# Between two propagation steps of a graph network: two of five adjacency products ahead of the put-off tile's overflow check, and the first of them pinned behind its logits

## The chip, the cores and the metric

The kernel runs on one core of one Trainium2 chip. The metric is the device time of one launch in microseconds (us), of which lower is better. Before the change it is 3214.06 us, the median of three runs.

## What is computed

The reference is a stack of four graph layers over 4096 nodes with 256 features each; after each layer comes a residual sum and a layer norm. The change lies in the second layer, which runs two steps. Each step multiplies the features by a row-normalised adjacency matrix (`R @ Xf`), and another copy of the features by an attention matrix cut to its top 90% of mass (`A @ Xa`).

```python
for n in range(2):
    q = Xa @ W1.T @ W2.T;  k = Xa @ W3.T
    probs = softmax(q @ k.T)
    A = probs with only the largest entries kept, whose sum reaches 0.9, rows summing to 1
    Xf = R @ Xf                      # R = (adj + I), rows summing to 1
    Xa = A @ Xa
    Z = Z + Xf @ U1[n].T + Xa @ U2[n].T
h = layernorm(X + Z)
```

## The kernel before

Rows are worked on in 32 tiles of 128 (`NT` is 32). For each tile, TensorE makes the logits against all 4096 keys in 8 chunks of 512 columns (L414), and ScalarE copies each chunk out of PSUM (L415). VectorE finds the largest values of each row (L433, then `tops`), ScalarE takes the exponential (L452 or L456), and VectorE's `pick` finds the threshold that leaves 90% of the mass.

In step 0 a row is expected to keep at most 16 entries, whose source rows are gathered by number with indirect DMAs on GpSimd's queue (L672). They are summed by matmuls with diagonal weights `dg` (VectorE L759, TensorE L761). Rows that keep more than that are entered into a list in DRAM. They are handled again at the end of the step, gathered into one full tile: the **put-off tile** (`put_off`, one tile in step 0, because `LATER[0]` is 1). It goes the dense way:

1. its list is loaded (SyncE L886), turned into row numbers (VectorE L888), and its rows are gathered (GpSimd L810, `xf_new`);
2. query (L394), logits (L414, L415), maximum (L433), exponential over the whole row (ScalarE L456), the 64 largest values (L528, L532), threshold (L550 to L564), which leaves a flag `bad_l` for each row;
3. the **overflow check**: a 1x1 matmul counts the flags (TensorE L588), ScalarE copies the count (L590), VectorE loads it into a register and branches around a slow search (L647, L648);
4. after the branch `settle` zeroes one group of surplus values (L658) and everything below the threshold (L663);
5. TensorE turns the cleaned row tile in chunks (L744), ScalarE copies (L747), TensorE multiplies by the features (L767), and the result is mixed, stored, and used for the keys and queries of step 1.

For a few more rows than the put-off tile holds there is a loop with a count known only at run time (`left_over`, L928). With this input it runs zero times, but all engines meet at it.

Step 1's adjacency products can start as soon as step 0's `Xf` is complete. `load_halves` loads it back from DRAM in eight pieces (SyncE L165, VectorE L150 and L152, ScalarE L151, tile `xh`). Five of the 32 products of step 1 stand between the steps. One product (`r_product`) is 8 calls of `neighbours`: SyncE fetches an 8-bit adjacency tile that serves two calls (L681, three buffers), ScalarE casts it (L683, two buffers `adjq`), and TensorE runs four matmuls (L686). After the last call a matmul with the identity closes the product (L688), and the result leaves by ScalarE (L705), VectorE (L706) and SyncE (L712). Successive products alternate between two PSUM banks.

The kernel is written against a scheduler. It takes instructions in the written order as priorities, and gives every engine an order fixed at build time. It may move an instruction ahead of ones written before it where its model of time finds a gap. It may not move instructions across a run-time branch that was written between them, so what is written before the check stays before it on every engine. `tc.keep_in_program_order(i)` takes that freedom from one instruction: it stays behind what was written before it on its engine.

The stages of the put-off tile are a generator; `advance(job)` runs it to its next `yield`. By the time the loop over tiles ends, it has been advanced twice (rows gathered, then query and logits). In the old version the remaining stages were all run by `finish`, below the five products. The third advance holds maximum, exponential, `tops`, `pick` and the check's matmul and copy; the fourth holds the register load, the branch and L654 to L658.

Of the kernel before, what the change touches and what calls it, by code (L numbers as in the profile page):

```python
# [56 lines left out]
def gnn_stack(ctx, tc, x, adjt, adjn, w0, b0, w1, w2t, w3t, u1t, u2t, ln_g, ln_b, w2, b2, w3, b3, out):  # L57
# [3 lines left out]
    nc = tc.nc  # L61
# [295 lines left out]
    with tc.tile_pool(name="l1", bufs=1, reuse_waits="tile") as l1:  # L357

        cur = {"late": False, "n": 0, "nef_done": False}


        FIRST = [[range(k * NT // 16, (k + 1) * NT // 16) for k in range(2)]]
# [311 lines left out]

        GP = LC // P

        def neighbours(n, i, g, acc_r, pn, xf):

            if g % 2 == 0:
                cur["a8"] = cur["w"].tile([P, 2 * GP, P], F8, tag="adj8", name="adj8", bufs=3)  # L680
                nc.sync.dma_start(cur["a8"], adj8_d[i][:, g * GP : (g + 2) * GP, :])  # L681
            a = cur["w"].tile([P, GP, P], F32R, tag="adjq", name="adjq", bufs=2)
            nc.scalar.copy(a, cur["a8"][:, g % 2 * GP : (g % 2 + 1) * GP, :])  # L683
            for j in range(GP):
                jt = g * GP + j
                nc.tensor.matmul(acc_r, a[:, j, :], xf[:, jt, :], start=(jt == 0), stop=False)  # L686
            if g + 1 == NLC:
                nc.tensor.matmul(acc_r, ident_r, xf[:, i, :], start=False, stop=True)  # L688
            if pn is not None:
                if g % (NLC // 2) == 0:  # L690
                    cur["b8"] = cur["w"].tile([P, NT // 2, P], F8, tag="adjn8", name="adjn8", bufs=2)
                    nc.gpsimd.dma_start(cur["b8"], adjn[i, :, g * GP : g * GP + NT // 2, :])
                k = g % (NLC // 2) * GP
                for j in range(GP):
                    jt = g * GP + j
                    nc.tensor.matmul(pn[:, :P], cur["a8"][:, g % 2 * GP + j, :], cur["b8"][:, k + j, :], start=(jt == 0),
                                     stop=(jt == NT - 1))

        def r_acc(i):

            return ps_acc.tile([P, 512], F32, tag=("acc", "nef")[i % 2 if cur["nef_done"] else 0], name="acc_r", bufs=1)

        def r_end(i, acc_r, pn):
            xf_new = work.tile([P, D], F32, tag="xf_new", name="xf_new", bufs=1)
            nc.scalar.activation(xf_new, acc_r[:, :D], AF.Copy, scale=rs[:, i : i + 1])  # L705
            nc.vector.scalar_tensor_tensor(xf_new, acc_r[:, D:], rs[:, i : i + 1], xf_new, op0=ALU.mult, op1=ALU.add)  # L706
            if pn is not None:

                junk = spare_row.bitcast(F32)[:, :P]
                nc.vector.scalar_tensor_tensor(junk, pn[:, :P], 1.0, ident, op0=ALU.mult, op1=ALU.mult,  # L710
                                               accum_out=nef[:, i : i + 1])
            nc.sync.dma_start(rows(xf_d, i), xf_new)  # L712

        def r_product(n, i, xf):

            acc_r, pn = r_acc(i), None
            if n == 0:
                pn = ps_acc.tile([P, 512], F32, tag="nef", name="nef_ps", bufs=1)
            for g in range(NLC):
                neighbours(n, i, g, acc_r, pn, xf)  # L720
            r_end(i, acc_r, pn)

        def pieces(n, st, nxt, ops, rs_now=()):
# [27 lines left out]
            for g in range(NLC):  # L751
                if nxt is not None:
                    logits_chunk(nxt["e"], nxt["q"], g)
                if few:
                    per = KEPT // NLC
                    for k in range(g * per, (g + 1) * per):
                        if k % 4 == 0:
                            dg = cur["w"].tile([P, 4, P], F32, tag="at", name="dg", bufs=2)
                            nc.vector.tensor_mul(dg, ident[:, None, :].to_broadcast([P, 4, P]),  # L759
                                                 st["w"][:, k : k + 4, None].to_broadcast([P, 4, P]))  # L760
                        nc.tensor.matmul(acc_a, dg[:, k % 4, :], st["G"][k], start=(k == 0), stop=(k == KEPT - 1))  # L761
                elif st is not None:
                    if g + 1 < NLC:
                        turn(g + 1)
                    for j in range(G):
                        jt = g * G + j
                        nc.tensor.matmul(acc_a, ats[g][:, j, :], cur["xa"][:, jt, :], start=(jt == 0),  # L767
                                         stop=(jt == NT - 1))
                if with_r:
                    neighbours(n, i, g, acc_r, pn, cur["xf"])  # L770
                for f in ops.get(g, ()):
                    f()
            if st is None:
                for i in rs_now:
                    r_product(n, i, cur["xf"])
            else:
                xa_new = work.tile([P, D], F32, tag="xa_new", name="xa_new", bufs=1)
                nc.scalar.activation(xa_new, acc_a, AF.Copy, scale=st["sc"])
                if n + 1 < STEPS:
                    put(xa_d, st, xa_new)  # L780
                st["xa"] = xa_new
# [11 lines left out]
        def fetch(n, st):  # L793

            i = st["tile"]
            for key, src in (("xf", xf_d), ("res", h_d if n else x1_d), ("x1", x1b_d)):
                if n == 0 and (key == "x1" or key == "res" and i is not None):
                    continue
                if i is None:
                    st[key] = gathered(src, st, key)  # L800
                else:
                    st[key] = work.tile([P, D], F32, tag=key, name=key, bufs=1)
                    nc.sync.dma_start(st[key], rows(src, i))
            if n == 0 and i is not None:
                st["res"] = cur["xa"][:, i, :]
# [136 lines left out]
        def run_step(n, es):  # L942
# [6 lines left out]
            jobs = []  # L949

            def advance(job):

                cur["late"] = True
                st = next(job["stages"], "end")
                cur["late"] = False
                if st == "end":
                    return True
                if st is not None:
                    job["st"] = st
                return False  # L960
# [19 lines left out]
            for i in range(-2, NT):  # L980
# [21 lines left out]
                if 0 < i + 2 < NT - 1:  # L1002
                    turned = []
                    g = 1 if n else 6
# [40 lines left out]
            if n == 0:  # L1045
                for fs in last:
                    for f in fs:
                        f()
                last = []
                cur["late"] = True  # L1050
                fetch(n, jobs[0]["st"])
                cur["late"] = False
                cur["nef_done"] = True
                for i in range(FIRST[1][0][0]):
                    r_product(1, i, cur["next"])
            todo = []
            if n > 0:
# [172 lines left out]
```

## Time and profile before

| what | value |
|---|---|
| runs | 3208.3, 3214.06 and 3225.59 us, median 3214.06 |
| profiled execution | 3106.69 us, of which the span is 3105.0 us |
| granted TensorE clock, mean | 0.976 |
| TensorE matmul busy | 2902.2 us, 93% of the span |
| VectorE, ScalarE, GpSimd busy | 2253.7, 1725.0 and 779.8 us |
| from the end of step 0's loop to step 1's first logits | about 1187 to 1300 us of the span |

The span is the time from the first to the last instruction. "PE" is TensorE's matmuls, "PEld" its weight loads, "DVE" VectorE, "ACT" ScalarE, "POOL" GpSimd, "SP" SyncE. A name such as "DVE e L663" is the engine, the tile that is written, and the source line. The granted clock is the share of full speed at which TensorE was allowed to run.

### The profile page before, as it was taken

The numbers are of one execution on the slowest core, as the hardware profiler recorded it, in microseconds if no ns is written. First come the engines' busy times: TensorE is split into PE (matmuls) and PEld (weight loads), VectorE is DVE, ScalarE is ACT, GpSimd is POOL, SyncE is SP. The second block draws the span as 40 slices with busy tenths as digits, with TensorE's granted clock in tenths as the row PEclk, the third lists the DMA queues.
The fourth block names the chain that finished last, engine by engine and source line by source line (L and its number), as shares of the span: only waits on it lengthen the run. The fifth ranks groups of instructions, "written<-read, shape, count | busy, mean of one in ns | idle before, by whom it ended". The sixth has DMA issues, their size and how long they took to land. (4 is left out here: it accounts for less than half of the span.)

```text
span 3105.0 us, 45412 instructions
## 1 busy us (share of the span) xinstructions
PE 2902.2 (93%) x14244; PEld 2300.0 (74%) x14244; DVE 2253.7 (73%) x7159; ACT 1725.0 (56%) x2883; POOL 779.8 (25%) x908
## 2 busy tenths in 40 slices
PE   7999889999999997799999999999999978999998
PEld 3788677788878875577777877878878546777886
DVE  4666688888888884379997999959998725443444
ACT  2555566666666655364555555546554426666664
POOL 1111167777777772000000000010001110000000
PEclk9999999999999998899999999999999998999999
DMA  9996378888878873310000111101111324333332
GB/s 170 158 176 136 66 131 138 164 153 154 147 153 155 161 149 112 117 50 25 25 21 25 37 34 38 30 31 35 39 35 32 115 88 152 107 107 97 107 107 78
DMA packets 247484, 299.44 MB, mean 96 GB/s; under 512 B 34464, under 2 KB 201312, under 8 KB 247232
## 3 DMA queue, kind: packets, MB, share of 16 engines
q0 software_dynamic: 46336, 104.28, 23.8%
q1 hardware_dynamic: 188656, 180.93, 18.9%
q10 hardware_dynamic: 12240, 11.23, 1.1%
q8 instruction: 115, 1.88, 0.3%
q14 instruction: 137, 1.12, 0.2%
HBM read 330.65 MB, written 66.32 MB: 128 GB/s over the span
## 5 line engine op out<-in xcount | busy, mean ns | idle before, releaser
L686 PE MATMUL acc_r<-xh,adjq 128*128 128x512 f32 x2048 | 617.1, 430 | 20.9 <-ACT adjq L683 12.0
L767 PE MATMUL acc_bank<-xa,at 128*128 128x256 f32 x2240 | 548.1, 385 | 25.8 <-ACT at L747 25.4
L672 POOL DMA_INDIRECT G<-x_d,cols x512 | 496.6, 970 | 214.4 <-PE acc_bank L761 77.6
L683 ACT CAST adjq<-adj 128x512 fp32r<-128x512 fp8e4 x512 | 316.2, 620 | 399.5 <-PE acc_r L686 318.8
L767 PEld LDWEIGHTS acc_bank<-xa,at 128*128 128x128 f32 x2240 | 408.4, 192 | 84.3 <-ACT at L747 37.1
L686 PEld LDWEIGHTS acc_r<-xh,adjq 128*128 128x128 f32 x2048 | 378.9, 191 | 110.4 <-ACT adjq L683 31.8
L433 DVE MAX8 cand<-e 128x8 f32<-128x228 f32 (+1 forms) x1088 | 386.6, 399 | 71.1 <-ACT e L415 69.5
L199 POOL TENSOR_TENSOR rstd<-ve,mhalf 128x1 f32<-128x1 f32 x166 | 100.3, 604 | 1330.9 <-DVE ve L197 1287.5
L415 ACT COPY e<-lg 128x512 f32<-128x512 f32 x544 | 315.0, 585 | 183.7 <-PE lg L414 179.9
L414 PE MATMUL lg<-kS,q 128*128 128x512 f32 x1088 | 385.0, 439 | 0.1
L1110 ACT CAST a<-a 128x1024 fp32r<-128x1024 fp8e4 x256 | 268.1, 1049 | 167.9 <-PE acc L175 127.9
L761 PE MATMUL acc_bank<-G,dg 128*128 128x256 f32 x1024 | 272.2, 387 | 12.5 <-DMA adj<-adj_d 5.4
L530 DVE FIND_INDEX8 cols<-top,e 128x8 uint32<-128x4096 f32 x64 | 282.8, 4419 | 0.0
L175 PE MATMUL acc<-xh,a 128*128 128x512 f32 x1024 | 261.9, 410 | 21.0 <-DMA x2i<-x_d 17.1
L175 PE MATMUL acc<-y0h,a 128*128 128x512 f32 x1024 | 250.0, 398 | 0.0
L175 PEld LDWEIGHTS acc<-xh,a 128*128 128x128 f32 x1024 | 193.5, 192 | 67.7 <-ACT xh L151 22.2
L175 PE MATMUL acc<-yh,a 128*128 128x512 f32 x1024 | 237.9, 394 | 0.0
L761 PEld LDWEIGHTS acc_bank<-G,dg 128*128 128x128 f32 x1024 | 196.6, 193 | 49.5 <-DVE dg L759 10.0
L175 PEld LDWEIGHTS acc<-yh,a 128*128 128x128 f32 x1024 | 192.3, 188 | 43.6
L175 PEld LDWEIGHTS acc<-y0h,a 128*128 128x128 f32 x1024 | 188.1, 188 | 38.8 <-issue 0.6
L747 ACT COPY at<-at_ps 128x512 f32<-128x512 f32 x288 | 168.8, 588 | 83.0 <-PE at_ps L744 81.3
L414 PEld LDWEIGHTS lg<-kS,q 128*128 128x128 f32 x1088 | 180.1, 192 | 20.4 <-ACT e L415 6.4
(287 smaller groups left out, 4430.3 us busy)
## 6 DMA issues: line engine op xcount, KB each, us to landing
adj<-adj_d SPq DMA_DIRECT2D x256, 128.0 KB
a<-adj_d SPq DMA_DIRECT2D x256, 128.0 KB
a<-in_adjt POOLq DMA_DIRECT2D x64, 256.0 KB
adj_d<-a SPq DMA_DIRECT2D x64, 256.0 KB
adjn<-in_adjn POOLq DMA_DIRECT2D x64, 256.0 KB
x_d<-x SPq DMA_DIRECT2D x64, 128.0 KB
xf_d<-xf_new SPq DMA_DIRECT2D x64, 128.0 KB
xf<-xf_d SPq DMA_DIRECT2D x64, 128.0 KB
```

Source lines behind the costliest of these rows:

```text
L175: nc.tensor.matmul(acc, a[:, j, :], halves(jt), start=(jt == 0), stop=(jt == NT - 1))
L414: nc.tensor.matmul(pl[:, :LC], q[k], kS[:, s], start=(k == 0), stop=(k == 1))
L415: nc.scalar.copy(l[:, s], pl[:, :LC])
L433: nc.vector.max(dst[:, 8 * g : 8 * g + 8], src[:, g * w : min((g + 1) * w, N)])
L530: nc.vector.max_index(st["at"][:, 8 * r : 8 * r + 8], t8, st["e"][:, :N])
L672: nc.gpsimd.indirect_dma_start(out=g, out_offset=None, in_=x1_d, in_offset=bass.IndirectOffsetOnAxis(ap=st["at"][:, k : k + 1], axis=0))
L683: nc.scalar.copy(a, cur["a8"][:, g % 2 * GP : (g % 2 + 1) * GP, :])
L686: nc.tensor.matmul(acc_r, a[:, j, :], xf[:, jt, :], start=(jt == 0), stop=False)
L747: nc.scalar.copy(at[:, :G, :], ps[:, :G, :])
L761: nc.tensor.matmul(acc_a, dg[:, k % 4, :], st["G"][k], start=(k == 0), stop=(k == KEPT - 1))
L767: nc.tensor.matmul(acc_a, ats[g][:, j, :], cur["xa"][:, jt, :], start=(jt == 0), stop=(jt == NT - 1))
L1110: nc.scalar.copy(a, a8)
```

## The change

Of the five products, the first two stay ahead of the put-off tile's next two stages, and the other three are written behind these. The branch thus stands, on every engine, behind two products instead of five. The first matmul of the first product is also pinned: it may not move ahead of what was written before it, the put-off tile's logits among that.

```diff
-        def neighbours(n, i, g, acc_r, pn, xf):
+        def neighbours(n, i, g, acc_r, pn, xf, pinned=False):
...
-                nc.tensor.matmul(acc_r, a[:, j, :], xf[:, jt, :], start=(jt == 0), stop=False)
+                first = nc.tensor.matmul(acc_r, a[:, j, :], xf[:, jt, :], start=(jt == 0), stop=False)
+                if pinned and jt == 0:
+                    tc.keep_in_program_order(first)
...
-        def r_product(n, i, xf):
+        def r_product(n, i, xf, pinned=False):
...
-                neighbours(n, i, g, acc_r, pn, xf)
+                neighbours(n, i, g, acc_r, pn, xf, pinned)
...
-                for i in range(FIRST[1][0][0]):
+                early = FIRST[1][0][0]
+                for i in range(early // 2):
+                    r_product(1, i, cur["next"], i == 0)
+                for _ in range(2):
+                    advance(jobs[0])
+                for i in range(early // 2, early):
                     r_product(1, i, cur["next"])
```

`early` is 5, so `early // 2` is 2. No arithmetic is added or removed: only the order of instructions differs, and only between the steps.

The orders that the scheduler gives before and after differ as follows.

- **TensorE.** Before, 16 of the first product's 32 matmuls L686 stood ahead of the run-time loop, 6 between the loop and the logits, and 10 behind the logits. After, all of them stand behind the logits. The check's matmul L588 stood behind the fifth product and now stands behind the second.
- **ScalarE.** The exponential L456 stood behind three casts L683 and the first product's L705, which followed the logits' copies; now no cast stands between the copies and the exponential. Two casts of the first product are made early in both orders. Four more stood ahead of the loop and one ahead of the logits' copies; now they stand behind the exponential.
- **GpSimd.** Before, the last four gathers L672 stood ahead of the put-off tile's `xf_new` and `res`. After: one gather, `xf_new`, one gather, `res`, two gathers. The last two gathers' matmuls now stand directly ahead of the logits on TensorE.
- **SyncE.** Of two adjacency tiles of the second product, one was fetched ahead of the loop and one right behind it; now both stand behind the last loads L165. Behind the loop the put-off tile's list is loaded ahead of `xf`, no longer after it.
- **VectorE.** L654 to L663 stood behind the fifth product's L706 and now stand behind the second's; L150 and L152 of the last pieces stand a little earlier against `dg` L759.

## The prediction

> **What bounds the kernel now.** The page comes first: TensorE is busy for 93% of the span, so a gain has to come from a stretch where it waits. The change reorders one such stretch, between the steps.
>
> ```profile
> PE 2902.2 (93%) x14244; PEld 2300.0 (74%) x14244; DVE 2253.7 (73%) x7159; ACT 1725.0 (56%) x2883; POOL 779.8 (25%) x908
> ```
>
> Next, who made TensorE wait between 1172 and 1306 us (total, number, longest). Four waits that the change can touch:
>
> ```profile
> PE at_ps L744 <- DVE e L663: 8.2, 1, 8.2
> PE acc_bank L761 <- DMA adj<-adj_d: 5.4, 1, 5.4
> PE acc_r L686 <- ACT adjq L683: 3.3, 1, 3.3
> PE tr L185 <- DMA xf_new<-x_d,from_l: 1.8, 1, 1.8
> ```
>
> The timelines show the largest. TensorE, then VectorE, ScalarE and GpSimd (start, length, what; in brackets the idle time before it and what ended it):
>
> ```profile
> 1217.97 7.51 PE L686 MATMUL acc_r<-xh,adjq 128*128 128x512 f32 x24 [3.27 <-ACT adjq L683]
> ...
> 1249.50 0.19 PE L588 MATMUL mm_bank<-ones_col,bad_l 128*1 128x1 f32 x2
> 1257.86 1.97 PE L744 MATMUL at_ps<-ident,e 128*128 128x128 f32 x8 [8.17 <-DVE e L663]
> 1259.65 3.70 PE L767 MATMUL acc_bank<-x,at 128*128 128x256 f32 x8
> ...
> 1265.79 1.89 PE L767 MATMUL acc_bank<-x,at 128*128 128x256 f32 x8
> ```
>
> ```profile
> 1220.53 0.16 DVE L564 SCALAR_TENSOR_TENSOR bad_l<-left_l,bad_l 128x1 f32<-128x1 f32 x1
> ...
> 1252.04 4.43 DVE L658 MATCH_REPLACE8 e<-match_l,e 128x4120 f32<-128x4120 f32 x1
> 1256.51 1.28 DVE L663 SCALAR_TENSOR_TENSOR e<-e,t_thr_l 128x1024 f32<-128x1024 f32 x1
> ```
>
> ```profile
> 1213.62 3.70 ACT L456 ACTIVATE e<-e,m_l 128x4096 f32<-128x4096 f32 x1
> ```
>
> ```profile
> 1191.71 0.94 POOL L672 DMA_INDIRECT G<-x_d,cols  x1 [20.58 <-ACT xh L151]
> ...
> 1195.84 0.95 POOL L672 DMA_INDIRECT G<-x_d,cols  x1 [0.30 <-issue]
> 1197.09 0.95 POOL L810 DMA_INDIRECT xf_new<-x_d,from_l  x1 [0.30 <-issue]
> ```
>
> The flags `bad_l` are ready at 1220.7, but their count L588 stands behind five products and runs at 1249.50. Only then do the branch, L658 and the first L663 run on VectorE, and TensorE sits idle for 8.17 us until 1257.86. VectorE was nearly idle for the 29 us before.
>
> **The change part by part.** All times are of the profiled execution.
>
> *Removed: the wait for the check, -8.2 us.* L588 now stands behind two products. VectorE needs from 1249.6 to 1261.3 for copy, branch, L658 and four L663, about 12 us; three products at 7.95 us (1225.56 to 1233.50 for one) cover that twice. Two checks of step 1 show that TensorE can work through a branch: VectorE's branch at 1868.77 lies inside TensorE work without a gap. Late next after this wait is the last product itself. The L706 now queued behind L658 and L663 on VectorE (the third product's) can be late by a few us; its bank is needed one product later, 8 us on, so it costs nothing.
>
> *Removed with it: a slow restart, -2.3 us.* After the idle time TensorE is slow. The busy-time table by stretch (length, PE busy, PEld, DVE, ACT, POOL, then granted clock, DMA share, GB/s):
>
> ```profile
> 1258.00:1263.00 5.00, 5.00 (x16) 4.16 (x17) 3.90 (x9) 1.17 (x2) 0.00 (x0) 0.50 0.01 3
> 1263.00:1278.00 15.00, 15.00 (x83) 13.11 (x82) 0.00 (x0) 3.51 (x6) 0.00 (x0) 1.00 0.00 1
> ```
>
> At 0.50 eight L767 take 3.70 us, at 1.00 1.89 us. From 1257.86 to the transposes of the result at 1277.91 are 20.05 us. At full clock I make it 17.7: 1.25 until the first L767 (transposes, one ScalarE copy), eight times 1.73 for L767 between starts, six times 0.43 for L744. The Trainium skill has a rule for it ("TensorE: Matmul & The Clock Gate", section "Why this matters for your kernels"): no idle gap over about 3 us between bursts of matmuls, or the clock falls to half. By the wait row alone the removal is worth 8.2 us, with the rule 10.5; the clock column decides for 10.5. The same rule speaks against the change where it makes a gap longer: see the stall below. There the 3.27 us stall before 1217.97 already brought half clock (24 matmuls take 7.5 us, against 5.8 at 0.24 each), and a stall of about 4 us costs one such phase again. I charge no second one; if it lasted one product longer, it would cost 2 us more.
>
> *Moved: the first product loses its cheap places, +8.0 us behind the stall.* Before, 22 of its 33 matmuls ran in gaps ahead of the logits and 11 after them, and another 8 of the second product before the stall. After, 8 (two chunks already cast) run between logits and stall. So before, 124 matmuls remain from 1217.97 to the end of the fifth product; after, 157. The 33 extra at 0.24 us are 8.0 us.
>
> *Moved: the logits come earlier, -5.0 us.* Four steps:
> 1. The meeting at the run-time loop ends at 1186.6 with the landing of a load L165 (issued 1182.63). Nothing in the change touches it. In the old order TensorE arrived last, at 1184.8; its jump took 3.57 us, and it restarted at 1190.21, which the waits' table books as "adj" DMA. With no product ahead of the loop it arrives near 1172, jumps while waiting, and starts at the first `dg`, 1188.1: 2.1 us earlier.
> 2. GpSimd's first gather then starts at 1189.6, and its issues follow every 1.25 us: `xf_new` at 1190.9 (its row numbers are ready near 1190.3), the last gather at 1195.85, as before. On GpSimd's queue `xf_new` passes three gathers, and two gathers fall behind `xf_new` and `res`.
> 3. The first logits now wait for that last gather, no longer for `xf_new`. The five issues from 1191.71 on took 2.7 to 4.5 us from start to landing; I take 3.75, so landing at 1199.6 and first logits at 1200.0, against 1204.10: -4.1 us. The diagonal `dg` and the last loads L165 come out near 1197, so they are covered by this landing.
> 4. The exponential no longer stands behind three casts and L705 (0.9 us between VectorE's maximum at 1212.7 and 1213.62). So it starts 5.0 us earlier, at 1208.6, takes 3.8, and the next cast and its first matmul come 0.66 later, as they did at 1217.3: 1213.0 against 1217.97. TensorE has run out of cast tiles near 1208.6, so it stalls about 4.4 us where it stalled 3.27. That is included in 1213.0.
>
> SyncE's queue: two adjacency fetches move from 1182 and 1188 to near 1213.5 and 1216. The nearest row (issued 1211.42, landed 1213.67) gives 2.3 us, and six more cast chunks of 1 us lie ahead of their use: covered, and without that cover 2 us. Loading the list ahead of `xf` gains about 0.4 us, which is inside the landing's uncertainty. The pinning itself issues nothing.
>
> Sum: -8.2 - 2.3 + 8.0 - 5.0 = -7.5 us. The profiled execution goes from 3106.69 to 3099.2. The timed median 3214.06 is 107 us (3.5%) above the profiled execution, and the profile does not show in what; I carry the difference over in us: 3206.6. The unknown is the landing of step 3: at 2.7 us the sum is -8.5, at 4.5 it is -6.8, and at 12.4, the longest flight of the gathers just before the loop (issued 1168.33, landed 1180.77, beside loads L165), it is +1.2.
>
> **The rivals.**
>
> *The logits gain nothing.* If gathers and loads land so late that logits start at 1204.1 again, 4.1 us are lost: -3.4, so 3210.7. For it: the landings just before the loop took 11 to 12 us (gathers; the load L165 issued at 1167.18 landed at 1177.85). Against: at 1189 the queues have drained.
>
> *Slower: the last gather holds up everything.* Place: the last gather's matmul, now directly ahead of the logits on TensorE. Its landing delays logits, exponential and all five products one for one. The kernel is slower from a flight of 11.3 us on (3.75 + 7.5). For it: six gathers and two half-megabyte loads now fall into 1189 to 1197, where the last load waited until 1195.88; the Trainium skill ("Trainium Kernel Development and Optimization", Key Constraints) says that the DMAs of all queues run on the same 16 engines and interleave. Against it: the busy-time table gives a DMA share of 0.40 for 1187 to 1204, and 12.4 is the longest flight seen here, at a share of 0.61. With 16 us, an estimate beyond it, it would be +4.8: 3218.9.
>
> *More than the profile shows.* Timed executions are 107 us longer; if a part of that lies in waits such as these, the gain grows. No row supports it beyond that difference. I price it at a gain of 20 us, an estimate: 3194.
>
> *The change does not do what it says.* The order rules that out: L588 stands behind two products and the three others behind it.
>
> **How the numbers follow.** Chances: the sum 0.60, logits gain nothing 0.12, slower 0.06, more than shown 0.22. The likeliest is 3206.6, its own range 3198 to 3215 (landing 1 us either way, and the scatter of the three runs, half of 17 us). Without 2 in 10 at the ends: 3192 to 3218. About 0.5% (16 us) is what a measurement of this kernel can tell from no change. Over 0.5% faster: 0.15 of the first case by scatter, 0.05 of the second, 0.8 of the fourth, together 0.27. Over 0.5% slower: half of the third and a little scatter, 0.05. The rest, 0.68, lies within.
>
> **What would show it.** Right: L744 follows the fifth product with no idle time, its first L767 take 1.9 us, L588 runs near 1229 and L663 ends before 1243; first logits near 1200, `adjq` stall of 4 to 5 us before 1213, fifth product's end near 1252.5 (3 us later than now), transposes of the result near 1270.4. Wrong: a wait of L744 for L663, a half clock after it, logits at 1204 or later with a wait on a gather, or a gain beyond 12 us in this stretch.

## The result, and the profile after

| | before | after |
|---|---|---|
| median of 20 runs each | 3213.76 us | 3206.49 us |
| range | 3207.04 to 3225.59 | 3199.99 to 3222.28 |
| ratio of after to before | | 0.9979, 95% interval 0.9966 to 0.9991 |
| profiled execution (span) | 3106.69 us (3105.0) | 3209.68 us (3208.0) |

The kernel became 7.3 us faster by the medians: a small gain, but the interval lies below 1. The forecast median was 3206.6.

The two profiled executions themselves seem to say the opposite, since the span grew by 103 us. None of this lies between the steps; it is taken up below, where the kernel before is profiled again. All comparisons of stages therefore count from one event: the first DMA that SyncE issues once all engines have met at the run-time loop. I call it the meeting. The stretch that is compared ends with the transposes of the put-off tile's result. Meeting, first logits and end of the stretch, in before and then in after:

```profile
1187.17 0.32 SPq L803 DMA_DIRECT2D xf<-xf_d  x1
...
1204.10 1.09 PE L414 MATMUL lg<-kS,q 128*128 128x512 f32 x4
...
1277.91 0.38 PE L185 MATMUL tr<-ident,xf 128*128 128x128 f32 x2
```

```profile
1300.10 0.34 SPq L888 DMA_DIRECT2D to_l<-list_d  x1
...
1314.46 1.37 PE L414 MATMUL lg<-kS,q 128*128 128x512 f32 x4
...
1385.38 0.38 PE L185 MATMUL tr<-ident,xf 128*128 128x128 f32 x2
```

TensorE's waits between 1285 and 1420 us of after (total, number, longest), the ones that answer to those shown of before:

```profile
PE acc_bank L763 <- DVE dg L761: 12.7, 1, 12.7
...
PE acc_r L686 <- ACT adjq L683: 3.3, 1, 3.3
PE acc_bank L763 <- issue: 1.9, 1, 1.9
...
PE acc_bank L769 <- ACT at L749: 0.2, 1, 0.2
```

The row of 8.2 us for the check is gone. The 12.7 us are not new waiting: TensorE now has no product to run ahead of the meeting and stands there longer. The timeline of TensorE shows the same (start, length, what, and in brackets the idle time before it; lines from L688 on have moved down by two):

```profile
1322.44 2.10 PE L686 MATMUL acc_r<-xh,adjq 128*128 128x512 f32 x8
1327.86 7.50 PE L686 MATMUL acc_r<-xh,adjq 128*128 128x512 f32 x24 [3.32 <-ACT adjq L683]
...
1343.47 0.19 PE L588 MATMUL mm_bank<-ones_col,bad_l 128*1 128x1 f32 x2
...
1367.31 0.40 PE L690 MATMUL acc_r<-xh,ident 128*128 128x512 f32 x1
1367.56 1.03 PE L746 MATMUL at_ps<-ident,e 128*128 128x128 f32 x8
1368.83 1.99 PE L769 MATMUL acc_bank<-x,at 128*128 128x256 f32 x8 [0.24 <-ACT at L749]
```

L588 runs behind the second product, L746 follows the fifth without idle time, and the first eight L769 take 1.99 us instead of 3.70. VectorE does the check underneath. The first of the four L663 is shown here; the last ends at 1356.12, 11 us before TensorE needs it:

```profile
1346.35 4.43 DVE L658 MATCH_REPLACE8 e<-match_l,e 128x4120 f32<-128x4120 f32 x1
1350.82 1.28 DVE L663 SCALAR_TENSOR_TENSOR e<-e,t_thr_l 128x1024 f32<-128x1024 f32 x1
```

The granted clock (seventh figure, ahead of DMA share and GB/s) is 1.00 for the whole of the put-off tile's product, and 0.56 in the 3.86 us behind the stall:

```profile
1327.86:1331.72 3.86, 3.86 (x10) 3.04 (x11) 2.66 (x17) 1.78 (x4) 0.00 (x0) 0.56 0.13 34
1367.50:1385.30 17.80, 17.56 (x97) 15.35 (x96) 0.48 (x1) 5.03 (x9) 0.00 (x0) 1.00 0.02 8
```

### The profile page after: what moved, and what is told of

The parts are those of the page before. It is cut to its first block, busy times and chain, and to the rows that moved or that the text cites. A ratio compares the mean times of both kernels' runs of the same rounds, so it can differ in the third digit from the quotient of the medians.

```text
span 3208.0 us, 45408 instructions
## 1 busy us (share of the span) xinstructions
PE 2928.8 (91%) x14244; PEld 2304.8 (72%) x14244; DVE 2259.1 (70%) x7159; ACT 1729.5 (54%) x2883; POOL 781.5 (24%) x908
## 5 line engine op out<-in xcount | busy, mean ns | idle before, releaser
L686 PE MATMUL acc_r<-xh,adjq 128*128 128x512 f32 x2048 | 617.7, 431 | 16.9 <-ACT adjq L683 16.5
L769 PE MATMUL acc_bank<-xa,at 128*128 128x256 f32 x2240 | 547.7, 384 | 26.3 <-ACT at L749 25.9
L672 POOL DMA_INDIRECT G<-x_d,cols x512 | 500.7, 978 | 284.2 <-PE acc_bank L763 126.3
L683 ACT CAST adjq<-adj 128x512 fp32r<-128x512 fp8e4 x512 | 316.0, 620 | 421.7 <-PE acc_r L686 250.8
L769 PEld LDWEIGHTS acc_bank<-xa,at 128*128 128x128 f32 x2240 | 407.8, 192 | 85.3 <-ACT at L749 37.6
L686 PEld LDWEIGHTS acc_r<-xh,adjq 128*128 128x128 f32 x2048 | 379.7, 192 | 111.8 <-ACT adjq L683 38.2
L415 ACT COPY e<-lg 128x512 f32<-128x512 f32 x544 | 316.1, 587 | 223.6 <-PE lg L414 172.5
L175 PE MATMUL acc<-xh,a 128*128 128x512 f32 x1024 | 259.2, 406 | 20.6 <-DMA x2i<-x_d 16.2
L175 PEld LDWEIGHTS acc<-y0h,a 128*128 128x128 f32 x1024 | 187.9, 188 | 38.9 <-issue 0.6
```

Source lines behind the costliest of these rows:

```text
L175: nc.tensor.matmul(acc, a[:, j, :], halves(jt), start=(jt == 0), stop=(jt == NT - 1))
L415: nc.scalar.copy(l[:, s], pl[:, :LC])
L672: nc.gpsimd.indirect_dma_start(out=g, out_offset=None, in_=x1_d, in_offset=bass.IndirectOffsetOnAxis(ap=st["at"][:, k : k + 1], axis=0))
L686: first = nc.tensor.matmul(acc_r, a[:, j, :], xf[:, jt, :], start=(jt == 0), stop=False)
```

## The experiments

Theory A: the gain is the hidden check (8.2 us) with the restart at half clock behind it (about 2 us). The pin of the first product works against it: it puts 8 us of matmuls behind the stall and brings back less through earlier logits. Theory B, the main rival: the gain comes from the earlier logits, or from differences outside this stretch.

All timelines were read in the same way. Each row is one profiled execution; times are us. The columns are: from the meeting to the first logits; on to the end of the stall for `adjq`; on to the end of the fifth product; from there (L588's start where it comes last) to the put-off tile's first L744 or L746; on to the transposes of its result; and the sum of these.

| kernel | logits | stall's end | fifth product | check | result | sum |
|---|---|---|---|---|---|---|
| before, first profile | 16.9 | 13.9 | 31.5 | 8.4 | 20.0 | 90.7 |
| before, second | 18.3 | 13.9 | 30.2 | 8.4 | 19.5 | 90.2 |
| after, first | 14.4 | 13.4 | 39.7 | 0 | 17.8 | 85.3 |
| after, second | 12.9 | 13.2 | 39.7 | 0 | 17.8 | 83.7 |
| split, no pin, first | 15.5 | 13.9 | 31.7 | 0 | 17.8 | 78.9 |
| split, no pin, second | 16.7 | 13.9 | 30.3 | 0 | 17.8 | 78.7 |
| pin, no split | 14.0 | 13.7 | 39.4 | 8.4 | 19.5 | 95.0 |
| after, own `dg` | 14.0 | 13.0 | 38.6 | 0 | 17.8 | 83.3 |
| before, filled wait | 15.3 | 13.9 | 31.4 | 8.4 | 17.9 | 86.8 |
| no pin, one product behind the check | 16.7 | 13.9 | 31.9 | 0.3 | 17.9 | 80.7 |
| no pin, quarters, first | 16.3 | 11.3 | 31.4 | 0 | 17.8 | 76.8 |
| no pin, quarters, second | 16.2 | 11.3 | 31.4 | 0 | 17.8 | 76.7 |
| pin, quarters | 12.9 | 10.7 | 38.9 | 0 | 17.8 | 80.4 |

The timed ratios below are against the kernel before on the same chip. They were taken in three groups (the first four, the next four, and the last three experiments), each on a chip of its own, where before had medians of 3217.92, 3201.14 and 3205.11 us. Lines of added code move the line numbers of a version; the tile names stay.

Outside the stretch nothing sets the versions apart. Ahead of it, from the end of the last logits of step 0's tile loop to the meeting, twelve profiles took 48.1 to 50.3 us, pinned or not (before's first, whose step 0 was faster, 44.7). From the meeting to the last instruction before took 1917.8 and 1916.6 us, after 1907.9 and 1908.4, the split without the pin 1903.3 and 1901.2, the pin without the split 1920.7. So the order of the versions is that of their stretches. The sizes are less sure there than in the stretch: step 1 alone, from its first logits to the end, varies from 1799.4 to 1804.5 us.

### The changed kernel once more

> The changed kernel, unchanged. Theory A (hidden check): the stretch from the end of the meeting at the run-time loop (SyncE's first issue behind it) to the transposes of the put-off tile's result takes 85.3 us again, L746 follows the fifth product without idle time, the stall ahead of the casts is 3.3 us, and the time is 7 us below before, ratio 0.998. Theory B (the gain comes from elsewhere, from the logits or from differences outside the stretch): the stretch varies by several us from execution to execution.

Measured: ratio 0.9982 (0.9970 to 0.9995), median 4.5 us below before. The stretch took 83.7 us, 1.6 less than in the first profile, all of it ahead of the logits. The columns that the split bears on repeat within 0.1 us (no wait for the check, 39.7 us of products, 17.8 us to the result). The variation that theory B speaks of is there, but it is 1 to 2 us and sits nearly all in one column.

### Split without the pin

> The changed kernel without the pin: products split 2 and 3 around the check, but the first product free to run in gaps ahead of the logits, as before. Theory A: the removed wait (8.2 us) and the slow restart (2.3 us) are the whole gain and the pin costs more than it brings; stretch 90.7 - 10.5 = 80.2 us, total 10 to 10.5 us below before (ratio 0.9967), 3 to 5 us faster than the changed kernel; first logits near 17 us behind the end of the meeting. Theory B, gain from the earlier logits: without the pin nothing is left but the hidden check, at most 3 us below before, slower than the changed kernel.

```diff
-                    r_product(1, i, cur["next"], i == 0)
+                    r_product(1, i, cur["next"])
```

Measured: ratio 0.9970 (0.9958 to 0.9983), and 78.9 us for the stretch. TensorE of this version:

```profile
1320.71 7.47 PE L686 MATMUL acc_r<-xh,adjq 128*128 128x512 f32 x24 [3.28 <-ACT adjq L683]
1328.02 0.40 PE L690 MATMUL acc_r<-xh,ident 128*128 128x512 f32 x1
1328.35 0.19 PE L588 MATMUL mm_bank<-ones_col,bad_l 128*1 128x1 f32 x2
...
1352.46 1.03 PE L746 MATMUL at_ps<-ident,e 128*128 128x128 f32 x8
```

These 24 matmuls are what is left of the second product: the first one and 8 matmuls of the second ran before the stall. In after, the 24 matmuls at 1327.86 only finish the first product, and the second follows in full (39.7 against 31.7 us to the end of the fifth). Against before, this version gains 11.5 us in the stretch (90.5, the mean of two, to 78.9); after gains 6.0 (to 84.5). Theory B is refuted for the logits: without their gain the kernel is faster. By the timed runs of the two versions alone the difference is less firm: 7.1 us between the medians of 22 runs each, but the intervals of the two ratios overlap. The trace decides here.

### The pin without the split

> The kernel before with the pin alone: all five products stay ahead of the check, the first one pinned behind the logits. Theory A: first product behind the stall +8.2, logits and stall -3.0, meeting -1.7; total +3 to +5 us against before (ratio 1.001 to 1.0015); the wait of L746 for L663 stays at 8.2 us and eight L769 behind it take 3.7 us. Theory B: 3 to 7 us faster than before, by the earlier logits.

```diff
-                early = FIRST[1][0][0]
-                for i in range(early // 2):
-                    r_product(1, i, cur["next"], i == 0)
-                for _ in range(2):
-                    advance(jobs[0])
-                for i in range(early // 2, early):
-                    r_product(1, i, cur["next"])
+                for i in range(FIRST[1][0][0]):
+                    r_product(1, i, cur["next"], i == 0)
```

Measured: ratio 1.0009 (0.9993 to 1.0025), so no slowdown is proved by time alone. The stretch took 95.0 us, 4.5 more than before, and the wait of the check stands as it did:

```profile
1381.18 1.97 PE L746 MATMUL at_ps<-ident,e 128*128 128x128 f32 x8 [8.17 <-DVE e L663]
1382.97 3.17 PE L769 MATMUL acc_bank<-x,at 128*128 128x256 f32 x8
```

The eight L769 were expected to take 3.7 us; here the half clock ended, by the trace's clock records, 4.2 us behind the first L746, in before's first profile 5.3 us behind the first L744. Logits 14.0 instead of 17.6 us behind the meeting, first five products 39.4 instead of 30.9: the pin costs 8.6 and brings 3.6 plus 0.2. It loses in the stretch.

### The kernel before, profiled again

> The kernel before, unchanged, for a second profile of it. If the 107 us between the first profile and the timed runs lie in one fast execution of step 0's loop, the span is near 3212 us here, with about 54 us for two tiles in step 0 as in the changed kernel's profile, and the stretch between the steps takes 90.7 us again, with 8.2 us of wait for L663. If they lie in waits between the steps (the rival that forecast more than the profile shows), the stretch is longer than 90.7 us here.

Measured: a span of 3215.8 us with the stretch at 90.2 us, and TensorE's wait for the check is the same to the hundredth (8.17 us; the table of waits rounds it):

```profile
PE at_ps L744 <- DVE e L663: 8.2, 1, 8.2
```

So the 107 us between the first profile and the timed runs do not lie between the steps. They lie in step 0: from its first logits copy to its last (L415) are 781.5 us in before's first profile and 891.3 in this one. The busy-time tables of before's first profile and of its second over the middle of step 0 (length, then TensorE's matmuls):

```profile
500.00:1100.00 600.00, 599.62 (x3412) 480.05 (x3411) 525.53 (x1564) 388.58 (x759) 442.66 (x469) 1.00 0.84 153
```

```profile
540.00:1210.00 670.00, 619.65 (x3393) 484.12 (x3393) 533.52 (x1565) 393.28 (x764) 440.31 (x464) 0.98 0.76 137
```

About the same work (3412 and 3393 matmul records) takes 600 us without a gap in the first and 670 us with 50 us of gaps in the second. Measured from logits copy to logits copy, two tiles take 49.1 us on average in the first profile of before and 53.4 to 56.1 us in the other twelve profiles of this study (tiles 2 to 30). The rival "more than the profile shows" loses its reason: waits between the steps do not grow in this second profile.

### The last diagonal in memory of its own

In after's first profile, TensorE stands still for 1.85 us between the gathers' matmuls, just ahead of the logits, while VectorE makes the fourth `dg` behind an L150 that waits for a load:

```profile
1309.44 0.69 DVE L150 TENSOR_SCALAR e<-e 128x1024 int32<-128x1024 int32 x1 [1.31 <-DMA e<-xf_d]
1310.05 0.68 DVE L761 TENSOR_TENSOR dg<-ident,w 128x512 f32<-128x512 f32 x1
```

> The changed kernel, with the fourth diagonal dg of the last tile in memory of its own (half of spare_row), so that VectorE can make it ahead of the last two L150, which wait for loads. Theory C (it was this dg and not the last gather's landing that held the logits): the idle 1.85 us of TensorE behind the first three groups of gathers shrinks or goes, the first logits come 1 to 2.6 us earlier than 14.4 us behind the end of the meeting, and the total is 1 to 2 us below the changed kernel. Rival D (the last gather's landing holds them): TensorE waits for G, logits at 14.4 again, no gain.

```diff
-                            dg = cur["w"].tile([P, 4, P], F32, tag="at", name="dg", bufs=2)
+                            if st["tile"] == NT - 1 and k == KEPT - 4:
+                                dg = spare_row.bitcast(F32)[:, 4 * P : 8 * P].rearrange("p (a b) -> p a b", b=P)
+                            else:
+                                dg = cur["w"].tile([P, 4, P], F32, tag="at", name="dg", bufs=2)
```

Measured: first logits at 14.0 us, between the 14.4 and 12.9 of after; ratio 0.9985 (0.9972 to 0.9998), not to be told from after's. The wait on `dg` is gone, and a wait on the gathers has come in its place (the diagonal is now called `spare_row`):

```profile
1285.16 0.70 PE L766 MATMUL acc_bank<-G,spare_row 128*128 128x256 f32 x2 [0.33 <-DMA G<-x_d,cols]
...
1287.45 0.70 PE L766 MATMUL acc_bank<-G,spare_row 128*128 128x256 f32 x2 [0.72 <-DMA G<-x_d,cols]
```

Both theories were half right: the diagonal held TensorE, and the last gather's landing lies so close behind it that removing the one wait gains nothing that can be told from the scatter. This last gather was issued at 1284.48 us and its matmul began at 1287.45: at most 3.0 us, where the prediction took 3.75. In the five profiles with the pin the landing of this gather is recorded 2.7 to 2.9 us behind its issue.

### Before, with the wait filled

> The kernel before, with 30 added matmuls behind the branch of the check (128x512, ident by xh, into a bank that is free; nothing uses the result), which fill TensorE's wait for L663 and change nothing else. Theory A1 (the slow restart comes from the idle time): the granted clock stays at 1.0, the first eight L767 of the put-off tile take 1.9 us, and the time from the first transposes to the transposes of the result is 17.7 instead of 20.05 us: 2.3 us below before in total. Rival (the restart is slow by itself, for its first waits on ScalarE's copies): 3.7 and 20 us as before, and no gain.

```diff
+            if not loop and cur["n"] == 0:
+                warm = ps_acc.tile([P, 512], F32, tag="nef", name="warm", bufs=1)
+                for j in range(30):
+                    nc.tensor.matmul(warm, ident_r, cur["next"][:, j, :], start=(j == 0), stop=(j == 29))
```

Measured: with 7.16 us of added matmuls inside the wait, L748 still starts 8.4 us behind L588, but the first eight L771 (L767 in before) run at full clock:

```profile
1347.34 7.16 PE L654 MATMUL warm<-xh,ident 128*128 128x512 f32 x30
1355.58 1.09 PE L748 MATMUL at_ps<-ident,e 128*128 128x128 f32 x8 [1.09 <-DVE e L667]
1356.91 1.99 PE L771 MATMUL acc_bank<-x,at 128*128 128x256 f32 x8 [0.24 <-ACT at L751]
```

From the first transposes to the result it takes 17.9 us, against 20.0 and 19.5 in before's two profiles: 1.7 to 2.2 us are the price of the idle time's clock, and they vanish although the work behind the check is the same, and TensorE still waits for VectorE and for ScalarE's copy. In total time the gain does not show: ratio 1.0005 (0.9984 to 1.0025), and an effect of 2 us (0.0006) is too small for this interval. The slow restart is shown by the trace alone.

### Only one product behind the check

> Without the pin, four products ahead of the check and only one behind it (8 us of cover). If the check needs about 12 us on VectorE from L588 to the first L663, as worked out in the prediction, one product leaves near 1 to 4 us of idle time at L746, and the total lies 0 to 4 us above the 2 and 3 split without the pin. If the cover needed is 8.2 us, as the wait row says, one product covers it nearly wholly, and the time is that of the 2 and 3 split.

```diff
-                for i in range(early // 2):
-                    r_product(1, i, cur["next"], i == 0)
+                for i in range(4):
+                    r_product(1, i, cur["next"])
...
-                for i in range(early // 2, early):
+                for i in range(4, early):
```

Measured: 0.33 us of idle time remains, full clock behind it, ratio 0.9968 (0.9955 to 0.9980), not to be told from the 0.9970 with three products behind (against before on another chip).

```profile
1349.32 1.09 PE L746 MATMUL at_ps<-ident,e 128*128 128x128 f32 x8 [0.33 <-DVE e L663]
```

So one product, 7.95 us by the prediction's lines, covers the check almost entirely. The prediction had worked out 12 us of VectorE work to cover; but L746 of the first chunk needs only the first of four L663, and the three others keep ahead of the chunks that use them (the first ends at 1349.26, the last at 1353.63, and TensorE waits for VectorE only once). The wait row, not the whole work behind the branch, gave the cover that is needed.

### The exponential in quarters

The stall ahead of 1217.97 in before is ScalarE's exponential of 3.7 us, behind which the casts of the adjacency wait. Here it is split, in the version without the pin, so that two casts can go between the quarters.

> Without the pin, split 2 and 3, and the put-off tile's exponential in four quarters in step 0 (with a sum over the four totals), so that the casts of the adjacency can go between them on ScalarE. Theory: the stall of TensorE for adjq (3.3 us, the length of the exponential) falls below 1.5 us and its half clock (1.5 us) goes with it; 3 to 4.8 us below the version without the pin, near 14 us below before (ratio 0.9957). Rival: the quarters only move the wait (casts queue behind the next quarter, each about 1 us), and the sum delays the check; no gain beyond 1 us.

```diff
+            elif cur["n"] == 0:
+                zq = small("zq", NQ)
+                for c in range(NQ):
+                    nc.scalar.activation(e[:, c * QW : (c + 1) * QW], e[:, c * QW : (c + 1) * QW], AF.Exp, bias=st["m"],
+                                         scale=1.0, accum_out=zq[:, c : c + 1])
+                nc.vector.tensor_reduce(z, zq, axis=AX.X, op=ALU.add)
```

Measured: ratio 0.9951 (0.9931 to 0.9970), stretch 76.8 us. ScalarE and TensorE:

```profile
1311.78 1.14 ACT L458 ACTIVATE e<-e,m_l 128x1024 f32<-128x1024 f32 x1
1312.83 0.19 ACT L458 ACTIVATION_READ_ACCUMULATOR e<-e,m_l 128x1 f32 x1
1312.91 1.13 ACT L689 CAST adjq<-adj 128x512 fp32r<-128x512 fp8e4 x2
1313.94 1.15 ACT L458 ACTIVATE e<-e,m_l 128x1024 f32<-128x1024 f32 x1
```

```profile
1313.58 4.28 PE L692 MATMUL acc_r<-xh,adjq 128*128 128x512 f32 x16 [0.71 <-ACT adjq L689]
1318.11 2.11 PE L692 MATMUL acc_r<-xh,adjq 128*128 128x512 f32 x8 [0.25 <-ACT adjq L689]
```

The stall falls from 3.3 to 0.7 us and no half clock follows. The stretch is 2.1 us shorter than without the quarters, less than the 3 to 4.8 expected. In "stall's end" 2.6 us are gained. The half clock, which I had counted as a saving of 1.5 us, saves less: the 24 matmuls behind the wait now take 6.6 us, against 7.5 at half clock without the quarters, since TensorE waits for a cast once more in between (0.25 us) and runs the 16 ahead of that a little slower; and in the second profile of the version without quarters there was no half clock at all, and they took 6.0.

### The last three on one chip

> The split without the pin once more, on the same chip as the next two, to see how far its stretch varies: 79 us from the end of the meeting to the transposes of the result, 10 us below before (ratio 0.997).

Measured: ratio 0.9951 (0.9932 to 0.9969), more than expected in time, but the stretch is 78.7 us, as expected. On this chip before itself ran from 3172 to 3225 us, so that the times of these three cannot rank them; the stretch can.

> The split without the pin and with the exponential in quarters once more: stretch near 77 us, 2 to 4 us below the version without the quarters, 13 to 15 us below before (ratio 0.9955).

Measured: ratio 0.9951 (0.9932 to 0.9970), stretch 76.7 us, the value of the first time within 0.1.

> The changed kernel with the exponential in quarters: pin, split and quarters. If the pin costs 33 matmuls of TensorE time whatever ScalarE does (8.2 us, against 2.7 us of earlier logits), it is 3 to 5.5 us slower than the version with quarters and no pin, stretch 80 to 82 us. If the pin's cost came only from products that queue up behind the whole exponential, the quarters take it away, and this version is the fastest, stretch 74 to 76 us.

Its edit is the quarters' diff above, made in the changed kernel. Measured: ratio 0.9947 (0.9924 to 0.9971), stretch 80.4 us. The pin costs 3.7 us here too: 7.6 in the column "fifth product", less 3.3 in "logits" and 0.6 in "stall's end". So the cost in "fifth product" does not come from products that queue up behind the whole exponential; it fits the 33 matmuls that lose their places in gaps (8 us at 0.24 each). Of all versions, the split without the pin and with quarters has the shortest stretch; it beats both given kernels by the stretch in both executions, and before by its timed interval.

## Why the prediction was right

*Removed, the wait for the check, -8.2 us: confirmed.* The row of 8.2 us stands in every profile with five products ahead of the check and nothing added (three), and in none with two (eight). That the L706 behind L658 on VectorE costs nothing is also confirmed: the five products run without a gap.

*Removed with it, the slow restart, -2.3 us: confirmed, a little smaller.* 17.8 us after, as forecast (17.7), but 20.0 and 19.5 before: 1.7 to 2.2 us, as in the experiment with the filled wait. By the clock records the half clock reached 5.3 us past the first transposes in before's first profile and 4.2 in its second.

*The first product loses its cheap places, +8.0 us: confirmed.* 39.7 us against 31.5 and 30.2, so +8.2 to +9.5. What the forecast missed is that half clock behind the stall comes and goes: it is in before's first profile and not in its second. Part of the 9.5 us is that; where both versions have it, the first product costs 8.2.

*The logits come earlier, -5.0 us: right as a mean, missed in the first profile.* To the stall's end before took 30.8 and 32.1 us, after 27.8 and 26.2: -4.5 between the means, but -3.0 between the two first profiles. The steps of it:
1. TensorE's restart 2.1 us earlier: first `dg` 3.0 us behind the meeting before, 1.05 after. Confirmed.
2. GpSimd's issues: last gather at 9.2 us behind the meeting instead of the forecast 8.7, since the six issues followed every 1.3 us and not every 1.25. `xf_new` moved from 9.9 to 3.9 us (forecast 3.7).
3. First logits forecast at 12.8 us behind the meeting: 14.4 and 12.9 measured. This is the term that failed in the first profile. The prediction named the last gather as what comes last and called `dg` covered; the profile shows the fourth `dg` last (1310.05), and TensorE at half clock for the first 0.2 us of the logits and the 3.2 us before them. The two limits lie close together: with the wait on `dg` taken away, the last gather held TensorE, and the logits began at 14.0.
4. The exponential no longer behind the casts, -0.9: 9.0 and 8.9 us from logits to exponential instead of 9.5, so -0.6.

The stall was forecast to grow to 4.4 us and measured 3.32, because TensorE did not run out of cast tiles where the exponential began (1323.50) but a microsecond later: its last eight matmuls ahead of the stall run from 1322.44 to 1324.54. The two adjacency fetches moved on SyncE's queue cost nothing, as forecast: no product waits for `adj`.

*The rivals.* "The logits gain nothing" is refuted by the first column. "Slower through the last gather" is refuted for the executions seen: the flight is near 3 us. "More than the profile shows" lost its reason (see before, profiled again). The carrying over of 107 us in absolute terms was right, since they lie in step 0, which the change does not touch.

The sum was -7.5 us. The stretch shows -6.0 (means of two profiles each): -8.4 for the wait, -2.0 for the restart, +8.8 for the first product and -4.5 for what comes earlier, rounded. The timed medians show -7.3 and -4.5 in two comparisons. So the mechanism was right and every term within 1 us, but three of the four came out a little worse than forecast. That the first timed difference lies within 0.2 us of the sum is luck: the interval of its ratio reaches from 3 to 11 us.

## What to carry over

A cheap check that ends in a run-time branch should be written where other engines still have one product of work behind it; here the wait row of the first TensorE instruction that needs the work behind the branch told how much that must be. Before keeping a second edit that comes with such a change, run it alone: here the pin moved the logits forward as meant, and cost two to three times what it brought, since work that ran in gaps had to be done on the path. And compare stages from a common event, not whole spans: two profiled executions of one kernel differed by 111 us, in a stage that no edit touched.

## What the runs showed of the hardware

*The clock at the edge of a stall.* A stall of TensorE of 3.0 to 3.3 us was followed by half clock in 8 of 10 profiles and not in the other two; a stall of 0.7 to 0.8 us never (three profiles), and 8.2 us of idle time always (three). Before's two profiles have the same stall of 3.27 us. The 24 matmuls behind it take 7.51 us in the first (shown with the prediction) and 6.03 us in the second:

```profile
1331.30 6.03 PE L686 MATMUL acc_r<-xh,adjq 128*128 128x512 f32 x24 [3.27 <-ACT adjq L683]
```

In the trace's clock records around this stretch each half-clock phase lasts 3.41 us or a multiple of it (10.24 us around the wait for the check), whatever the work. The Trainium skill ("TensorE: Matmul & The Clock Gate", section "What's actually happening") says why that would be so: activity is judged in windows of about 3.4 us that run freely and don't start with the work. The durations here fit it, and so do the places. Lay windows of 3.41 us out from the boundaries in the clock records: in each of the eight profiles one window held 2.3 to 3.0 us of the stall, and the half clock began at that window's end; in the two others a boundary fell into the middle of the stall, and each window held 1.6 to 1.7 us of it. So it was the place of the stall against the windows that decided, and not its length. The prediction's rule, no gap over about 3 us, is too simple for a stall of this length. For a forecast it means that such a stall costs its half clock (24 matmuls in 7.5 us instead of 6.0) with a chance, not for certain.

*Step 0 has no single speed.* Two tiles took 49.1 us in one profiled execution and 53.4 to 56.1 us in all others; TensorE had no idle time in 600 us of the first, and 50 us of it in 670 us of the second. GpSimd's gathers last the same in both (968 and 971 ns each), but GpSimd idles more per gather in the slower one (0.53 against 0.39 us), about half of it ahead of gathers that wait for TensorE's `acc_bank` matmuls:

```profile
L672 POOL DMA_INDIRECT G<-x_d,cols x394 | 381.2, 968 | 152.7 <-PE acc_bank L761 63.4 <-issue 34.3 <-PE acc_r L686 17.4
```

```profile
L672 POOL DMA_INDIRECT G<-x_d,cols x345 | 334.9, 971 | 184.4 <-PE acc_bank L761 90.0 <-issue 60.4 <-PE lg L414 11.6
```

(First before's first profile, then its second, both from 500 to 1100 us; number of gathers, busy time, mean ns, idle time and its releasers.) What slows the ring of gathers and matmuls in most executions stays open; no run here was made to find it. Between these two executions it is worth 110 us, more than ten times the change studied.
